# A decoder layer on one core: two softmax copies moved to ScalarE, FFN weights loaded within the attention, last sums closed in PSUM

## The chip, the core and the metric

The kernel runs on one core of one Trainium2 chip. The metric is the device time of one execution in microseconds. The engines are TensorE (PE; its weight loads are PEld), VectorE (DVE), ScalarE (ACT), GpSimd (POOL) and SyncE (SP), which here issues nearly all DMAs. [...]

## The reference

Two batches of 512 tokens, D = 1024, all in float32. Three sublayers, each followed by a layer norm over the sum with its input:

```python
# 1. causal attention over a window of 128: 32 query heads, 8 kv heads, head size 128
s = einsum("bhgnd,bhmd->bhgnm", q, k) / sqrt(128)      # masked: j <= i and i - j < 128
o = softmax(s) @ v;  x = layernorm(x + o @ wo.T)
# 2. fake-quantised product with the context (8 bits, scale s, zero point z)
fq(x) = (clip(round(x / s + z), 0, 255) - z) * s
x = layernorm(x + fq(x) @ fq(ctx))
# 3. FFN with ternary weights, 2752 inner features
inter = silu(gate(x / 128)) * up(x / 128)
q = int8(trunc(clip(inter * 128, -128, 127)))
x = layernorm(x + int8(trunc(clip(down(q) * 128, -128, 127))))
```

## The kernel before

**Order.** The code is written as generators that are stepped from each other (`between` in `attention` and `feed_forward`, classes `Background` for work in the background); a framework then places every instruction in its engine's queue by expected readiness and adds the waits. Up to eight DMAs are in flight on SP, in eight lanes.

**Strassen.** Projections, output projection and gate/up products are done as seven products of half-size blocks. `strassen_left` (L87) makes sums of the weights (L93 to L96), `strassen_right` (L73) sums of the activations (L80 to L83); its third difference overwrites a quarter of its input. `strassen` (L100) runs products 1, 6, 2, 7, 5, 4, 3 of four matmuls each (L109); product 1 is copied by ACT (L115), product 2 as well (L121), the others are added by DVE (L118 to L134).

**Attention (L166), per batch and kv head group g, 16 groups.** While group m's four token tiles are worked, the projections of group m + 1 are stepped in between. A tile takes: scores of four heads (`scores`, L268) into PSUM tile `ps`, the 128 keys of the tile before and its own; DVE copies the earlier keys (L284) and copies its own under the mask (L285), takes the maximum (L289), ACT the exponent with its sum (L293), DVE scales (L299). `transpose_p` (L302): PE transposes the weights into PSUM tile `pt` (L305), DVE multiplies them by the mask keep_cur (L311, part of the own keys) and by keep_prev (L312, part of the earlier keys). `weigh` (L317): two matmuls into `o` (L319, L321), ACT copies to `oT` (L325). After four tiles `keep` (L327) makes Strassen sums `oS` on DVE (L333 to L336) and stores them with five DMAs in `kept` (L340).

**In the background of the attention.** The sums of the output weights (`sum_output_weights`, L801, 32 steps) and of the gate/up weights (`sum_weights`, L826, 42 steps): a step loads a tile (two buffers), makes four sums on DVE into a tile `s`, and stores that with one DMA to DRAM (L823, L853). In batch 1's attention the output projection of batch 0 (`project_out`, L365, matmuls `y` at L412) and the cross attention of batch 0 (`Cross`, L441, with `quantise`, L470) run too.

**FFN (L540).** 21 units of 128 inner features and a rest of 64, for each batch. A unit loads its weights (`load_factors`, L561: two DMAs of weights, one of sums) and its down weights (`load_down`, L582, split in `split`, L590, into hi and lo of type f32r), makes gate and up by Strassen, `activate` (L598), and every second unit adds its down products (L656) to `acc` in SBUF on DVE (L662). Output and cross attention of batch 1 run in the background of batch 0's FFN. After the rest unit (`rest_unit`, L627) `finish` (L666) does each of four tiles: x is loaded back from DRAM (L671, one buffer fin_x) for batch 0, then ACT Abs and Sign (L676, L677), DVE (L679 to L684), ACT Square (L687), the root (L48), ACT scale (L693), output DMA (L694). The last two units (21st and rest) of batch 1 run in two halves of 256 tokens (L723 to L738).

Of the kernel before, what the change touches and what calls it, by code (L numbers as in the profile page):

```python
# [18 lines left out]
P = 128  # L19
# [3 lines left out]
D = 1024  # L23
# [49 lines left out]
def strassen_right(nc, pool, x, name):  # L73

    b11, b12, b21, b22 = (x[:, ts(k, KH), ts(n, NH)] for k in range(2) for n in range(2))
    t = pool.tile([P, 3, KH, NH], F32, tag="t", name=name)
    t1, t2, t4 = (t[:, k] for k in range(3))
    nc.vector.tensor_tensor(t1, b12, b11, ALU.subtract)  # L80
    nc.vector.tensor_tensor(t2, b22, t1, ALU.subtract)
    nc.vector.tensor_tensor(b12, b22, b12, ALU.subtract)
    nc.vector.tensor_tensor(t4, b21, t2, ALU.subtract)  # L83
    return b11, b21, b22, t4, t1, t2, b12
# [81 lines left out]
def attention(nc, tc, consts, xbuf, tpool, ps_p, dram, kept, complete, between):  # L166
# [3 lines left out]
    ident, mask_i, keep_cur, keep_prev = consts  # L170
    xT_d, wq_d, wk_d, wv_d = dram
    with ExitStack() as ctx:
# [44 lines left out]
        qT, kT, vT, v = {}, {}, {}, {}  # L217
# [34 lines left out]
        def transpose_v(b, g):  # L252
            ps = ps_t.tile([P, TPB, P], F32, tag="t", name=f"vtr_{b}_{g}")
            for i in range(TPB):
                nc.tensor.transpose(ps[:, i, :], vT[b, g][:, ts(i, P)], ident)
            v[b, g] = kvpool.tile([P, TPB, P], F32, tag="v", name=f"v_{b}_{g}")
            nc.scalar.copy(v[b, g], ps)

# [9 lines left out]
        def scores(b, g, i):  # L268
# [12 lines left out]
            if i == 0:  # L281
                nc.gpsimd.memset(s, MASKED)
            else:
                nc.vector.tensor_copy(s, ps[:, :, 0:P])  # L284
# [17 lines left out]
        def transpose_p(b, g, i, s):  # L302
            ps = ps_t.tile([P, G, P], F32, tag="t", name=f"pt_{b}_{g}_{i}")
            for h in range(G):
                nc.tensor.transpose(ps[:, h, :], s[:, h, :], ident)  # L305
            cur = work.tile([P, G, P], F32, tag="cur", name=f"cur_{b}_{g}_{i}", bufs=1)
            if i == 0:
                nc.vector.tensor_copy(cur, ps)
                return cur, None
            prev = work.tile([P, G, P], F32, tag="prev", name=f"prev_{b}_{g}_{i}", bufs=1)  # L310
            nc.vector.tensor_tensor(cur, ps, keep_cur.unsqueeze(1).to_broadcast([P, G, P]), ALU.mult)  # L311
            nc.vector.tensor_tensor(prev, ps, keep_prev.unsqueeze(1).to_broadcast([P, G, P]), ALU.mult)  # L312
            return cur, prev
# [3 lines left out]
        def weigh(b, g, i, cur, prev):  # L317
            ps = ps_o.tile([P, G, P], F32, tag="o", name=f"o_{b}_{g}_{i}")
            nc.tensor.matmul(ps, v[b, g][:, i, :], cur, start=True, stop=prev is None)  # L319
            if prev is not None:  # L320
                nc.tensor.matmul(ps, v[b, g][:, i - 1, :], prev, start=False, stop=True)  # L321
            if i == 0:
                outputs[b, g] = work.tile([P, 4, 2, NH], F32, tag="oT", name=f"oT_{b}_{g}")
            half, place = divmod(i, 2)
            nc.scalar.copy(outputs[b, g][:, ts(half, 2), :, ts(place, P)], ps.rearrange("p (k j) t -> p k j t", k=2))  # L325

        def keep(b, g):  # L327

            o = outputs[b, g]
            a11, a12, a21, a22 = (o[:, k] for k in range(4))  # L330
            t = work.tile([P, 3, 2, NH], F32, tag="oS", name=f"oS_{b}_{g}", bufs=1)
            s4, s1, s2 = (t[:, k] for k in range(3))
            nc.vector.tensor_tensor(s1, a21, a22, ALU.add)  # L333
            nc.vector.tensor_tensor(s2, s1, a11, ALU.subtract)
            nc.vector.tensor_tensor(a21, a11, a21, ALU.subtract)
            nc.vector.tensor_tensor(s4, a12, s2, ALU.subtract)  # L336
            to = kept[b]
            for k, src in ((slice(0, 2), o[:, 0:2]), (slice(3, 4), o[:, 3:4]), (slice(4, 6), t[:, 1:3]),
                           (slice(6, 7), o[:, 2:3]), (slice(2, 3), t[:, 0:1])):
                nc.sync.dma_start(out=to[:, k, g], in_=src)  # L340
# [3 lines left out]
        for m, (b, g) in enumerate(groups):  # L344
# [4 lines left out]
            for i in range(TPB):  # L349
# [4 lines left out]
                cur, prev = transpose_p(b, g, i, s)  # L354
# [3 lines left out]
                weigh(b, g, i, cur, prev)  # L358
# [181 lines left out]
def feed_forward(nc, tc, xres, spill, x2T, tpool, gate_up, wd_d, pools, out, between):  # L540

    wgu_d, rest_d, sums = gate_up
    raw_pool = pools[1]
    with ExitStack() as ctx:
# [16 lines left out]
        def load_factors(u):  # L561

            m = units[u][1]
            w = wbig.tile([P, 7, KH, P], F32, tag="wbig", name=f"wgu_{u}")
            if m == NCHUNK:
                rest = w.rearrange("p a c i -> p (a c) i")[:, :KC]
                nc.sync.dma_start(out=rest, in_=rest_d)
                return rest
            nc.sync.dma_start(out=w[:, 0:2], in_=wgu_d[m, :, 0].rearrange("p (j c) i -> p j c i", j=2))
            nc.sync.dma_start(out=w[:, 2], in_=wgu_d[m, :, 1, KH:])  # L570
            nc.sync.dma_start(out=w[:, 3:7], in_=sums[m])
            return [w[:, k] for k in (0, 1, 6, 2, 3, 4, 5)]

        def load_tail():
# [5 lines left out]
            left[u + 1] = load_factors(u + 1)  # L580
# [67 lines left out]

        def down(us, i, e):
# [4 lines left out]
            parts = [(acts[v], half) for v in us for half in halves[v]]  # L654
            for k, (act, half) in enumerate(parts):
                nc.tensor.matmul(ps, act[:, ts(i, P)], half[:, ts(e, HALF)], start=k == 0, stop=k == len(parts) - 1)  # L656
# [6 lines left out]
            if us[-1] % PER == NCHUNK and e == 1:  # L663
                finish(t)

        def finish(t):  # L666

            y = acc[t]
            if t in spill:
                x = work.tile([P, D], F32, tag="fin_x", name=f"fin_x_{t}", bufs=1)  # L670
                nc.sync.dma_start(out=x, in_=spill[t])  # L671
            else:
                x = xres[t]
            a = wdp.tile([P, D], F32, tag="wd", name=f"fin_{t}", bufs=1)
            r = raw_pool.tile([P, D], F32, tag="raw", name=f"fin_r_{t}")
            nc.scalar.activation(a, y, AF.Abs, scale=128.0)  # L676
            nc.scalar.activation(y, y, AF.Sign)  # L677

            nc.vector.tensor_scalar(r, a, 128.0, RND, ALU.min, ALU.add)  # L679
            nc.vector.scalar_tensor_tensor(a, r, RND, a, ALU.subtract, ALU.is_gt)  # L680
            nc.vector.scalar_tensor_tensor(r, r, RND, a, ALU.subtract, ALU.subtract)
            nc.vector.tensor_tensor(r, r, y, ALU.mult)
# [4 lines left out]
            nc.scalar.activation(y, x, AF.Square, bias=mean, accum_out=total)  # L687
# [8 lines left out]
        left[0] = load_factors(0)  # L696
        right, todo = {}, []
        for u, (b, m) in enumerate(units[:split_at]):
            load_down(u)
            if u + 1 < split_at:  # L700
                left[u + 1] = load_factors(u + 1)
            else:
                load_tail()
            if m == 0:
                right[b] = strassen_right(nc, tpool, x2T[b], f"t2_{b}")
            if m == NCHUNK:
                rest_unit(u, b)
# [15 lines left out]
        for h in range(2):  # L723
            where = [(i, e) for i in range(h * TPB // 2, (h + 1) * TPB // 2) for e in range(2)]
            for u in range(split_at, len(units)):
                if h == 0:
                    load_down(u)
                if u == len(units) - 1:
                    rest_unit(u, 1, h)
                else:  # L730
# [3 lines left out]
                    todo = []  # L734
                if h == 0:
                    split(u)
            for i, e in where:
                down((split_at, split_at + 1), i, e)  # L738
# [3 lines left out]
def decoder_layer(ctx, tc, x, xT, ctx_kv, wq, wk, wv, wo, s1, z1, s2, z2, wgu, wgu_rest, wd, out):  # L742
# [25 lines left out]
    keep_prev = const.tile([P, P], F32, tag="keep_prev", name="keep_prev")  # L768
    nc.gpsimd.affine_select(
        out=keep_prev, in_=ones, compare_op=ALU.is_gt, fill=0.0, base=0, pattern=[[-1, P]], channel_multiplier=1  # L770
    )
# [18 lines left out]
    x2T, sums, complete = {}, [], set()  # L790
    wo_sums = scratch.tile([P, 4, NKV, 2, HALF], F32, tag="wo_sums", name="wo_sums")
# [9 lines left out]
    def sum_output_weights(pool):  # L801
# [10 lines left out]
        for n, (g, j, q) in enumerate(steps):  # L812
# [4 lines left out]
            t = pool.tile([P, 4, Q4], F32, tag="s", name=f"wo_sum_{g}_{j}_{q}")  # L817
            t4, t1, t2, t3 = (t[:, k] for k in range(4))
            nc.vector.tensor_tensor(t1, b12, b11, ALU.subtract)
            nc.vector.tensor_tensor(t2, b22, t1, ALU.subtract)  # L820
            nc.vector.tensor_tensor(t3, b22, b12, ALU.subtract)
            nc.vector.tensor_tensor(t4, b21, t2, ALU.subtract)
            nc.sync.dma_start(out=wo_sums[:, :, g, j, ts(q, Q4)], in_=t)  # L823
            yield

    def sum_weights(pool):  # L826
# [13 lines left out]
        for n, (m, k) in enumerate(steps):  # L840
# [6 lines left out]
            s = pool.tile([P, 4, 2, P], F32, tag="s", name=f"sum_{m}_{k}")  # L847
            s1_, s2_, s3_, s4_ = (s[:, q] for q in range(4))
            nc.vector.tensor_tensor(s1_, a21, a22, ALU.add)
            nc.vector.tensor_tensor(s2_, s1_, a11, ALU.subtract)  # L850
            nc.vector.tensor_tensor(s3_, a11, a21, ALU.subtract)
            nc.vector.tensor_tensor(s4_, a12, s2_, ALU.subtract)
            nc.sync.dma_start(out=sums[m][:, :, k : k + 2], in_=s)  # L853
            yield

    def in_attention(b, g, i):
# [8 lines left out]
        if calls[0] % 3 == 0:  # L865
            aside.step()
        if calls[0] % 3 == 0 and (b or g or i):
# [3 lines left out]

    calls = [0]
    with tc.tile_pool(name="s_prep", bufs=2) as prep, tc.tile_pool(name="ps_y", bufs=2, space=PSUM) as ps_y:
        ahead.add(sum_output_weights(prep))
        ahead.add(sum_weights(prep))
        attention(nc, tc, (ident, mask_i, keep_cur, keep_prev), xbuf, tpool, pools[3],
                  (xT, wq, wk, wv), kept, complete, in_attention)
        aside.drain()
        ahead.drain()

# [5 lines left out]

    aside.add(cross.context(1))
    aside.add(cross_tokens(1))
    feed_forward(nc, tc, xres, spill, x2T, tpool, (wgu, wgu_rest, sums), wd, pools, out, in_feed_forward)
# [50 lines left out]
```

## Time and profile before

| | us |
|---|---|
| median of 3 runs | 2054.29 (2053.85 to 2056.23) |
| profiled execution | 2049.04 |
| its span | 2047.2 |
| PE busy in the span | 1963.9 |
| DVE busy | 1238.8 |
| ACT busy | 479.8 |
| mean DMA rate | 210 GB/s |

Stages in the trace: attention of batch 0 to about 500 us, of batch 1 to 1102, FFN of batch 0 to about 1660, its four finishes to 1735 beside the FFN of batch 1, which goes to 1999, then the tail. The profile is of one execution; times are from the start of its span. A group of instructions is one line and operation: busy time, mean duration in ns, then the idle time of its engine just before it and what ended that. A matmul of float32 is two passes on PE, so two records; 512 columns take 0.43 us a pass.

### The profile page before, as it was taken

The numbers are of one execution on the slowest core, as the hardware profiler recorded it, in microseconds if no ns is written. First come the engines' busy times: TensorE is split into PE (matmuls) and PEld (weight loads), VectorE is DVE, ScalarE is ACT, GpSimd is POOL, SyncE is SP. The second block draws the span as 40 slices with busy tenths as digits, with TensorE's granted clock in tenths as the row PEclk, the third lists the DMA queues.
The fourth block names the chain that finished last, engine by engine and source line by source line (L and its number), as shares of the span: only waits on it lengthen the run. The fifth ranks groups of instructions, "written<-read, shape, count | busy, mean of one in ns | idle before, by whom it ended". The sixth has DMA issues, their size and how long they took to land.

```text
span 2047.2 us, 21954 instructions
## 1 busy us (share of the span) xinstructions
PE 1963.9 (96%) x8016; PEld 1441.6 (70%) x8016; DVE 1238.8 (61%) x2435; ACT 479.8 (23%) x1121; POOL 14.4 (1%) x35
## 2 busy tenths in 40 slices
PE   8999999999999999999997999999999999999993
PEld 5877777778666666667774666666678877888882
DVE  5888787787334345345774443633467687666667
ACT  1222212222111122112332211211123245221224
POOL 0000000000000000000000000000000000000000
PEclk9999999999999999999998999999999999999997
DMA  8998887875466655655249865667733345534421
GB/s 286 323 321 286 258 264 242 279 239 183 180 251 227 223 213 216 235 213 188 108 152 323 307 248 213 245 223 261 257 113 122 126 147 193 192 132 149 149 83 41
DMA packets 218826, 430.57 MB, mean 210 GB/s; under 512 B 15072, under 2 KB 149216, under 8 KB 199008
## 3 DMA queue, kind: packets, MB, share of 16 engines
q1 hardware_dynamic: 217568, 427.09, 59.8%
q10 hardware_dynamic: 1152, 2.10, 0.3%
q8 instruction: 63, 1.03, 0.2%
q14 instruction: 43, 0.35, 0.0%
HBM read 354.68 MB, written 74.45 MB: 210 GB/s over the span
## 4 chain that ended last, share of the span: by engine, by line
PE 75%; DMA 12%; DVE 9%; SPq 2%; issue 1%; ACT 1%; DVEq 0%; ACTq 0%
PE prod L109 39%; PE y L412 17%; PE d L656 8%; PE ps L277 3%; DMA w<-in_wq_dram 3%; DMA or<-wo_sums 2%; PE o L319 2%; DMA raw<-in_wgu_dram 2%; PE o L321 1%; PE m L525 1%; DMA w<-in_wv_dram 1%; PE pt L305 1%; DMA or<-in_wo_dram 1%; SPq L836 1%; DMA wgu<-sums 1%
## 5 line engine op out<-in xcount | busy, mean ns | idle before, releaser
L412 PE MATMUL y<-or,ol 128*128 128x512 f32 x896 | 406.9, 595 | 16.9 <-DMA wgu<-in_wgu_dram 10.8
L109 PE MATMUL prod<-x2T,wgu 128*128 128x256 f32 x1312 | 304.6, 380 | 0.1
L412 PEld LDWEIGHTS y<-or,ol 128*128 128x128 f32 x896 | 167.4, 190 | 189.9 <-issue 173.8
L109 PEld LDWEIGHTS prod<-x2T,wgu 128*128 128x128 f32 x1312 | 249.3, 191 | 47.3 <-issue 13.1
L109 PE MATMUL prod<-xT,w 128*128 128x256 f32 x1128 | 268.9, 382 | 7.1 <-ACT st L115 6.5
L109 PEld LDWEIGHTS prod<-xT,w 128*128 128x128 f32 x1128 | 211.0, 191 | 46.1 <-ACT st L115 10.6
L109 PE MATMUL prod<-t,wgu 128*128 128x256 f32 x984 | 231.2, 379 | 3.4 <-DMA wgu<-sums 2.8
L109 PEld LDWEIGHTS prod<-t,wgu 128*128 128x128 f32 x984 | 186.3, 190 | 41.4 <-issue 15.3
L109 PE MATMUL prod<-t,s 128*128 128x256 f32 x752 | 180.2, 380 | 1.3 <-DVE kT L134 1.2
L656 PE MATMUL d<-hi,act 128*128 128x512 f32 x352 | 153.5, 436 | 10.8 <-DVE act L621 10.7
L109 PEld LDWEIGHTS prod<-t,s 128*128 128x128 f32 x752 | 141.1, 190 | 27.0 <-issue 5.2
L656 PE MATMUL d<-lo,act 128*128 128x512 f32 x352 | 140.3, 399 | 0.0
L293 ACT ACTIVATE s<-s,top 128x128 f32<-128x128 f32 x256 | 99.6, 390 | 173.2 <-DVE top L290 173.0
L662 DVE TENSOR_TENSOR acc<-d,acc 128x512 f32<-128x512 f32 x160 | 110.1, 690 | 49.2 <-PE d L656 48.9
L124 DVE TENSOR_TENSOR st<-prod,st 128x256 f32<-128x256 f32 x88 | 37.0, 420 | 126.9 <-PE prod L109 126.5
L277 PE MATMUL ps<-kT,qT 128*128 128x256 f32 (+1 forms) x512 | 111.6, 354 | 0.0
L277 PEld LDWEIGHTS ps<-kT,qT 128*128 128x128 f32 x512 | 88.5, 190 | 28.9 <-issue 17.5
L594 ACT CAST hi<-wd 128x1024 fp32r<-128x1024 f32 x44 | 46.0, 1047 | 266.9 <-PE d L656 167.6
L325 ACT COPY oT<-o 128x512 f32<-128x512 f32 x64 | 37.4, 584 | 277.7 <-PE o L321 163.9
L656 PEld LDWEIGHTS d<-hi,act 128*128 128x128 f32 x352 | 66.8, 190 | 48.9 <-DVE acc L662 21.3
L284 DVE COPY s<-ps 128x512 f32<-128x512 f32 x48 | 33.0, 687 | 99.4 <-PE ps L277 99.3
L109 PE MATMUL prod<-t,w 128*128 128x256 f32 x376 | 89.8, 381 | 2.8 <-DVE st L124 2.8
(184 smaller groups left out, 2223.2 us busy)
## 6 DMA issues: line engine op xcount, KB each, us to landing
or<-wo_sums SPq DMA_DIRECT2D x64, 1024.0 KB, 5.2
or<-in_wo_dram SPq DMA_DIRECT2D x48, 1024.0 KB, 5.5
wgu<-sums SPq DMA_DIRECT2D x41, 1024.0 KB, 7.4
w<-in_wq_dram SPq DMA_DIRECT2D x64, 512.0 KB, 4.7
ol<-kept SPq DMA_DIRECT2D x112, 256.0 KB, 2.9
raw<-in_wgu_dram SPq DMA_DIRECT2D x168, 128.0 KB, 3.8
sums<-sum SPq DMA_DIRECT2D x42, 512.0 KB, 4.1
wd<-in_wd_dram SPq DMA_DIRECT2D x42, 512.0 KB, 3.7
```

The source lines that it names most:

```text
L109: nc.tensor.matmul(ps, left[k - 1][:, c, :], right[k - 1][:, c, :], start=start and c == 0, stop=c == KH - 1, skip_group_check=True)
L124: nc.vector.tensor_tensor(u3, two, p1, ALU.add)
L277: nc.tensor.matmul(ps[:, h, :width], qT[b, g, h][:, ts(i, P)], kT[b, g][:, lo : lo + width], start=True, stop=True,)
L284: nc.vector.tensor_copy(s, ps[:, :, 0:P])
L293: nc.scalar.activation(s[:, h, :], s[:, h, :], AF.Exp, bias=top[:, h : h + 1], scale=QSCALE, accum_out=total[:, h : h + 1],)
L305: nc.tensor.transpose(ps[:, h, :], s[:, h, :], ident)
L319: nc.tensor.matmul(ps, v[b, g][:, i, :], cur, start=True, stop=prev is None)
L325: nc.scalar.copy(outputs[b, g][:, ts(half, 2), :, ts(place, P)], ps.rearrange("p (k j) t -> p k j t", k=2))
L412: nc.tensor.matmul(ps, left[:, c // 2, c % 2], right[:, c // 2, c % 2], start=k in (1, 6, 5) and s == 0 and c == 0, stop=s == LAST and c == 3,
L594: nc.scalar.copy(hi, raw[u])
L656: nc.tensor.matmul(ps, act[:, ts(i, P)], half[:, ts(e, HALF)], start=k == 0, stop=k == len(parts) - 1)
L662: nc.vector.tensor_tensor(acc[t][:, ts(e, HALF)], ps, acc[t][:, ts(e, HALF)], ALU.add)
```

## The change

- `scores`: the copy of the earlier keys goes to ACT. `transpose_p`: instead of the product with keep_prev, ACT copies the whole of `pt` to `both`; `weigh` takes v of the tile before times `both` plus (v of this tile less v of the tile before, `vd`) times `cur`. The mask keep_prev is gone; `vd` is made once a group on DVE.
- `strassen_right` writes its third difference in a tile of its own; the input stays whole.
- The sums of the weights: one of the four is written over the loaded tile, and each store is split into two DMAs.
- The attention output of a group is two tiles, one for each half of the tokens.
- The weights of the FFN's first unit are loaded within the attention of batch 1, into the buffer of xT, and strassen_right of batch 0's FFN input is called there too. Before the first units of batch 1 the background queues are drained and batch 1's sums are made ahead of the rest unit.
- `finish` gets x and its sums handed in, x comes into the two buffers `right`, and Sign, rounding and comparison are in BF16 tiles.
- In the two last halves the sum is closed in PSUM: an identity matmul brings `acc` in, the 21st unit's down products are added ahead, the rest unit's come last, and `finish` reads PSUM.

```diff
 def strassen_right(nc, pool, x, name):
-    t = pool.tile([P, 3, KH, NH], F32, tag="t", name=name)
+    t = pool.tile([P, 4, KH, NH], F32, tag="t", name=name)
...
-    nc.vector.tensor_tensor(b12, b22, b12, ALU.subtract)
+    nc.vector.tensor_tensor(t3, b22, b12, ALU.subtract)
...
             v[b, g] = kvpool.tile([P, TPB, P], F32, tag="v", name=f"v_{b}_{g}")
             nc.scalar.copy(v[b, g], ps)
+            vd[b, g] = kvpool.tile([P, TPB - 1, P], F32, tag="vd", name=f"vd_{b}_{g}")
+            nc.vector.tensor_tensor(vd[b, g], v[b, g][:, 1:], v[b, g][:, : TPB - 1], ALU.subtract)
...
-                nc.vector.tensor_copy(s, ps[:, :, 0:P])
+                nc.scalar.copy(s, ps[:, :, 0:P])
...
-            prev = work.tile([P, G, P], F32, tag="prev", name=f"prev_{b}_{g}_{i}", bufs=1)
+            both = work.tile([P, G, P], F32, tag="both", name=f"both_{b}_{g}_{i}", bufs=1)
             nc.vector.tensor_tensor(cur, ps, keep_cur.unsqueeze(1).to_broadcast([P, G, P]), ALU.mult)
-            nc.vector.tensor_tensor(prev, ps, keep_prev.unsqueeze(1).to_broadcast([P, G, P]), ALU.mult)
+            nc.scalar.copy(both, ps)
...
+                nc.tensor.matmul(ps, v[b, g][:, i - 1, :], both, start=True, stop=False)
+                nc.tensor.matmul(ps, vd[b, g][:, i - 1, :], cur, start=False, stop=True)
...
+            if place == 0:
+                outputs[b, g, half] = work.tile([P, 2, 2, NH], F32, tag=f"oT{half}", name=f"oT_{b}_{g}_{half}", bufs=2 - half)
...
+def load_factors(nc, w, gate_up, m):
...
+    nc.sync.dma_start(out=w[:, 0:2], in_=wgu_d[m, :, 0].rearrange("p (j c) i -> p j c i", j=2))
+    nc.sync.dma_start(out=w[:, 2], in_=wgu_d[m, :, 1, KH:])
+    nc.sync.dma_start(out=w[:, 3:7], in_=sums[m])
+    return [w[:, k] for k in (0, 1, 5, 2, 3, 4, 6)]
...
             if us[-1] % PER == NCHUNK and e == 1:
-                finish(t)
+                x = stream.tile([P, 2, 2, HALF], F32, tag="right", name=f"fin_x_{t}").rearrange("p a b c -> p (a b c)")[:, :D]
                 nc.sync.dma_start(out=x, in_=spill[t])
+                finish(t, x, [acc[t]])
+
+        def finish(t, x, sums):
             a = wdp.tile([P, D], F32, tag="wd", name=f"fin_{t}", bufs=1)
-            r = raw_pool.tile([P, D], F32, tag="raw", name=f"fin_r_{t}")
-            nc.scalar.activation(a, y, AF.Abs, scale=128.0)
-            nc.scalar.activation(y, y, AF.Sign)
-            nc.vector.tensor_scalar(r, a, 128.0, RND, ALU.min, ALU.add)
-            nc.vector.scalar_tensor_tensor(a, r, RND, a, ALU.subtract, ALU.is_gt)
-            nc.vector.scalar_tensor_tensor(r, r, RND, a, ALU.subtract, ALU.subtract)
-            nc.vector.tensor_tensor(r, r, y, ALU.mult)
+            rm = raw_pool.tile([P, 2, D], BF16, tag="raw", name=f"fin_r_{t}")
+            r, m = rm[:, 0], rm[:, 1]
+            sign = b_work.tile([P, D], BF16, tag="a1", name=f"fin_s_{t}", bufs=1)
+            for k, y in enumerate(sums):
+                part = ts(k, D // len(sums))
+                nc.scalar.activation(a[:, part], y, AF.Abs, scale=128.0)
+                nc.scalar.activation(sign[:, part], y, AF.Sign)
+            nc.vector.tensor_scalar(r, a, RND, RND, ALU.add, ALU.subtract)
+            nc.vector.tensor_tensor(m, r, a, ALU.is_gt)
+            nc.vector.tensor_tensor(r, r, m, ALU.subtract)
+            nc.vector.scalar_tensor_tensor(r, r, 128.0, sign, ALU.min, ALU.mult)
...
             if m == NCHUNK:
+                finish_between()
+                right[b + 1] = strassen_right(nc, tpool, x2T[b + 1], f"t2_{b + 1}")
                 rest_unit(u, b)
...
+                    rest_unit(u, 1, h)
+                    for k, (i, e) in enumerate(where):
+                        pool, tag = (ps_d, "d") if k < 2 else (ps_p, "p")
+                        ps[i, e] = pool.tile([P, HALF], F32, tag=tag, name=f"d_{h}_{k}")
+                        nc.tensor.matmul(ps[i, e], ident, acc[TPB + i][:, ts(e, HALF)], start=True, stop=False)
+                        down_parts(ps[i, e], [split_at], i, e, False, False)
...
             for i, e in where:
-                down((split_at, split_at + 1), i, e)
+                down_parts(ps[i, e], [split_at + 1], i, e, False, True)
+                if e == 1:
+                    finish(TPB + i, xres[TPB + i], [ps[i, 0], ps[i, 1]])
...
-            nc.vector.tensor_tensor(t3, b22, b12, ALU.subtract)
+            nc.vector.tensor_tensor(b12, b22, b12, ALU.subtract)
             nc.vector.tensor_tensor(t4, b21, t2, ALU.subtract)
-            nc.sync.dma_start(out=wo_sums[:, :, g, j, ts(q, Q4)], in_=t)
+            nc.sync.dma_start(out=wo_sums[:, 0:3, g, j, ts(q, Q4)], in_=t)
+            nc.sync.dma_start(out=wo_sums[:, 3, g, j, ts(q, Q4)], in_=b12)
...
-            nc.vector.tensor_tensor(s3_, a11, a21, ALU.subtract)
+            nc.vector.tensor_tensor(a21, a11, a21, ALU.subtract)
             nc.vector.tensor_tensor(s4_, a12, s2_, ALU.subtract)
-            nc.sync.dma_start(out=sums[m][:, :, k : k + 2], in_=s)
+            nc.sync.dma_start(out=sums[m][:, 0:3, k : k + 2], in_=s)
+            nc.sync.dma_start(out=sums[m][:, 3, k : k + 2], in_=a21)
...
             aside.step()
+            if b and g == NKV - 1 and (0, "tokens") in complete and not early:
+                prepare_feed_forward()
...
+    def prepare_feed_forward():
+        w = xbuf.tile([P, 7, KH, P], F32, tag="x1", name="wgu_0")
+        early.append(load_factors(nc, w, gate_up, 0))
+        early.append(strassen_right(nc, tpool, x2T[0], "t2_0"))
...
+    def finish_between():
+        behind.drain()
+        aside.drain()
```

In the changed kernel the copy for `scores` is L285, the scaling L300, `both` L313, Abs and Sign of `finish` L691 and L692, its DVE steps L694 to L699, Square L702, its last ACT step L708, the adds to `acc` L676, and the copy of product 1 L114.

## The prediction

> **What bounds the kernel now.** I read the page first: its span, its busy times and its slices.
>
> ```profile
> span 2047.2 us, 21954 instructions
> PE 1963.9 (96%) x8016; PEld 1441.6 (70%) x8016; DVE 1238.8 (61%) x2435; ACT 479.8 (23%) x1121; POOL 14.4 (1%) x35
> ...
> PEclk9999999999999999999998999999999999999997
> ```
>
> TensorE sets the time: it idles only 83 of 2047 us. None of the edits takes matmul work away (the tail adds some), so only those holes can give anything. Adding up the idle stretches in the trace gives 5.5 us at the start, 63.0 in gaps and 20.2 after the last matmul, out and end included. Where they lie, from the windows view (span, then busy PE, PEld, DVE, ACT, POOL with counts, PEclk, DMA share, GB/s):
>
> ```profile
> 100.00:200.00 100.00, 96.64 (x442) 78.26 (x441) 82.89 (x187) 25.23 (x87) 1.05 (x2) 1.00 0.92 304
> 200.00:300.00 100.00, 93.08 (x424) 73.50 (x423) 80.52 (x181) 20.22 (x76) 0.52 (x1) 1.00 0.82 260
> 500.00:700.00 200.00, 200.00 (x731) 133.12 (x730) 77.35 (x147) 26.60 (x98) 1.05 (x2) 1.00 0.58 211
> 1100.00:1200.00 100.00, 88.24 (x304) 57.73 (x303) 42.65 (x68) 20.24 (x28) 0.00 (x0) 0.95 0.80 288
> 2000.00:2047.00 47.00, 16.64 (x58) 12.06 (x56) 33.69 (x73) 22.32 (x32) 0.00 (x0) 0.69 0.11 45
> ```
>
> In the first attention (to 500 us) PE misses 3 to 7 us per 100 while DVE is about 80% busy and the DMA engines 70 to 92%; in the second (500 to 1100) almost nothing is missing. Then come one hole at 1102 and the tail. The chain of waits across 1102 (start, us, what):
>
> ```profile
> 1102.02 0.59 ACT oT L325
> ...
> 1105.29 3.53 DMA kept<-oS
> 1108.82 0.02 issue
> 1108.84 0.03 SPq L569
> 1108.86 0.03 issue
> 1108.89 3.78 DMA wgu<-in_wgu_dram
> 1112.67 0.10 issue
> 1112.77 2.04 PE y L412 x2
> ```
>
> The last head's output is stored, and only behind that store does SP issue the first FFN weights: PE stands 10.79 us.
>
> **Early FFN weights (and boundary order): about -10.** Trace first: after the gap, one y matmul (two passes, 0.86 us elsewhere) and one product (1.73) take from 1112.77 to 1117.18, 4.41 instead of 2.59: 1.8 lost. So this place costs 12.6. The Trainium skill, "TensorE: Matmul & The Clock Gate" (Part 1), says that an idle window of some 3.4 us halves the clock until about as long has been worked. By it a rest below 3.4 us is free of that charge. The row agrees: after a 2.12 us gap at 1709.9, 14 matmuls took 3.26 us (14 x 0.216 is 3.02).
> In the changed order unit 0's weights are issued on SP within the last group, and its first products are mixed with the last tiles. After the last o matmul PE has ready: a product (1.73), a y step (3.43), four products (6.9): 12.1 us. Unit 1's weights still queue on SP behind the last stores. DVE has two quantise steps of raw_5 (0.81, 0.69) ahead of or among the oS sums, so the last store goes at about 5.9 instead of 3.3, lands 3.5 later, then wd and wgu: 9.5, plus 3.8 to 4.5 of landing, 13.3 to 14.1. Rest 1.2 to 2.0, with hand-overs 2 to 2.7 and no clock loss. Gain 12.6 - 2.5 = 10 (8 to 12; by the rule 1.8 less if the rest passes 3.4). The three loads moved early stand on SP some 16 places ahead of that group's first stores; their buffer (x1) held batch 1's xT, last read at 1059, so they wait for nothing then. Batch 0's strassen_right (four of 1.22 on DVE) stood at 1058 to 1066 before too: nothing.
>
> **Tail: about -3.** The act of the last half is ready at 2021.1. Before, eight more passes, the adds and Abs follow, and DVE's L679 starts at 2025.89. After, four f32r matmuls (0.43 each at the low clock) close tile 6 at 2022.9, half-width Abs/Sign (0.63 each) feed L694 at about 2024, and one add (0.69) no longer stands in the DVE chain: 1.9 + 0.6 = 2.5. Added: 8 identity matmuls x 0.86 = 6.9 us of PE; they lie in the gaps of 4.43 and 5.88 before 2013.55 and 2021.16, where PE waits for DVE's act. Uncovered they would cost 3.4 per half. BF16 in finish: the nearest rows (1.21 to 1.22 for L680 to L684) give nothing. The skill's "VectorE: DVE Perf Modes" (the perf-mode tier table) lets a tensor_tensor with all operands of 16 bits run twice as fast, which fits only L696: 0.5 per tile, up to 2.1 over four tiles. No run here shows it; I take a quarter, as other steps of the chain are on ACT. Sum 3 (0 to 5).
>
> **Finish of tiles 0 to 3, after unit 21: about +7.** Before, each tile waits for the one fin_x buffer, whose reload waits for the output's landing; that spreads the four tiles over 1662 to 1735 and costs PE 5 to 7 us there. With two reload buffers the tiles pack together. In ACT's changed order, between unit 22's g copy and the copy of product 1 of unit 23 (which PE's next accumulation needs) stand four Abs and four Sign (8 x 1.06), two Square (2 x 1.34), three table loads (3 x 1.28), two L708 (2 x 1.24), sigmoid, Abs and Sign of unit 22 (1.9): 19.8 us against 7.1 before. DVE has the matching chain. PE's work from the rest unit's start to where it needs that copy: 6.9 + 12.1 + 7.4 + 5.2 + 1.7 = 33.3 us; the finish chain begins when the first sums close and reaches the copy at about 42. Stall 8 to 9.4, plus some 2 of low clock and 1 to 2 of small waits, less the 5 to 7 saved: loss 7. Bounds: a gain of 3 if the chain keeps up, a loss of 10.
>
> **Softmax on ScalarE: about -8.** From the groups by form (busy, mean ns; idle before, releaser):
>
> ```profile
> L284 DVE COPY s<-ps 128x512 f32<-128x512 f32 x48 | 33.0, 687 | 99.4 <-PE ps L277 99.3
> L312 DVE TENSOR_TENSOR prev<-pt,keep_prev 128x512 f32<-128x512 f32 x48 | 32.6, 680 | 0.0
> L93 DVE TENSOR_TENSOR s<-w 128x512 f32<-128x512 f32 x47 | 32.4, 690 | 54.2 <-DMA w<-in_wv_dram 27.7 <-DMA w<-in_wq_dram 26.4
> ```
>
> DVE loses 48 x 0.687 (L284) and 48 x 0.680 (L312), 65.6 us; it gains 16 vd subtractions of 384 columns (between 0.42 and 0.69, say 0.55), 9. Net 57, half of it in the first attention: from 78 to 72% busy. ACT gains 96 x 0.584, 56 us, at 20% busy. `both` waits for DVE's cur on the same PSUM tile, so o starts 0.8 later than with prev; behind it on ACT stand oT and the next exp. PE has at least 1.7 us of other work between pt and o in nearly every tile: nothing, but up to 5 if a few lack it. Gaps named after softmax (`pt` behind L299) sum to 11; of the 20 us of gaps in 100 to 500 I take 8 (2 to 14).
>
> **Sums in place: about +8.** The fourth difference overwrites the loaded tile, so each of 74 steps issues a second store, and the buffer's next load waits for its landing. In SP's changed order about 50 such loads stand three DMAs or fewer behind their store (none before): SP stands still, and w, wo and raw loads queue behind it. DVE then waits at L93 or at the sums, with softmax behind it; it already waits 54 us for w (last row above). Replaying one stretch by hand (store 4.1, load 4.8, three sums 1.3, issue 0.4) gives 22 us for four steps, 5.5 each, if DVE takes each at once; queued on DVE about 6.5. Before, the 74 steps ran from 22 to 482 us, 6.2 each; the changed order ends them near 507, 6.55 each. So it is on the edge: 8, between 0 and 26.
>
> **x2T kept whole:** the same four DVE operations into one tile more; batch 1's four (4.9 us) now stand ahead of the rest unit, where PE has its 6.9: nothing.
>
> **Sum:** -10 - 3 + 7 - 8 + 8 = -6. The profiled execution took 2049.04 (span 2047.2), so 2043; the median of the runs lies 5.25 above it, so 2048.
>
> **Rivals.** *A, everything shows:* DVE relief 14, sums free, finish even, boundary 11, tail 4: 29, so 2025. For it: PE's holes lie exactly where DVE is full. Against it: the SP queue and ACT's 19.8 us. *C, the finish eats the boundary:* the rest at the boundary is 4 to 5 with its clock loss, so 6 gained there, 3 in the tail, and the pile-up costs 10: about 2055, no change. *B, slower:* the two-buffer turn of the weight sums becomes the pace of the first attention. Place: 22 to 520 us, SP. Each step at 6.8 instead of 6.55 stretches it by 74 x 0.25 = 18; DVE's relief of 8 then repays nothing: 2054.3 - 13 + 7 + 18 = 2066. It decides from about 6.63 per step (74 x 0.08 eats the 6 gained). For it: DMA share 0.92 and landings of 4 to 6 us already. Against it: 5.5 if nothing queues. *That ACT only takes over what PE waits for* is in the low end of the 8.
>
> **Numbers.** Forecast (2039 to 2050) 0.35; A 0.16; C 0.17; B 0.32. A measurement tells about 0.2%, 4 us, from no change: faster 0.51, same 0.17, slower 0.32. The range 2026 to 2068 reaches into A and B, and leaves out half of A's lower part and B's tail, about 2 in 10.
>
> **What would show it.** Boundary: the 10.8 us wait before y at 1102 gone, a wait of 2 to 3 for wgu of unit 1. Finish: one PE wait of 8 or more behind ACT st in unit 23. Tail: no adds at the end, about 3 us shorter after the last rest unit. Attention: DVE near 72% to 500 us, fewer gaps behind L300; if B, long DVE waits for wo, raw and w, and the last sum well past 507. I am wrong if ACT's added copies make pt or o late, or if the sums set the pace.

## The result and the profile after

| | before | after |
|---|---|---|
| median, us | 2054.48 (2047.81 to 2060.79, 12 runs) | 2054.68 (2045.03 to 2059.53, 12 runs) |
| profiled execution | 2049.04 | 2045.03 |
| its span | 2047.2 | 2043.0 |

The ratio is 0.9995 with an interval of 0.9978 to 1.0012: -1 us, give or take 3.5. A second measurement (run c1 below) gave 1.0000 (0.9989 to 1.0010). So the change made no difference that can be measured. The profiled execution of after is its fastest of twelve; its 4 us less are not the verdict, but its stages can be compared.

The page of after, same rows as shown of before:

```profile
span 2043.0 us, 22124 instructions
PE 1968.4 (96%) x8022; PEld 1444.1 (71%) x8032; DVE 1183.1 (58%) x2347; ACT 531.5 (26%) x1223; POOL 14.2 (1%) x34
...
PEclk9999999999999999999999999999999999999998
```

DVE has 56 us less work and ACT 52 more, as the diff says, and TensorE's busy time is up by 4.5. The dip of the clock at the boundary (the 8 in the middle of before's row) is gone. The windows of after (span, busy PE, PEld, DVE, ACT, POOL with counts, PEclk, DMA share, GB/s), with 1600 to 1700 added; the last line is 1600 to 1700 of before:

```profile
100.00:200.00 100.00, 95.07 (x433) 75.89 (x432) 77.36 (x176) 30.97 (x97) 0.53 (x1) 1.00 0.89 290
200.00:300.00 100.00, 94.35 (x433) 75.36 (x433) 72.91 (x164) 26.81 (x88) 1.05 (x2) 1.00 0.78 251
1100.00:1200.00 100.00, 97.43 (x338) 62.58 (x337) 45.16 (x73) 23.36 (x39) 0.00 (x0) 1.00 0.80 299
1600.00:1700.00 100.00, 91.33 (x386) 72.83 (x386) 77.49 (x144) 44.20 (x64) 1.94 (x3) 0.97 0.41 141
2000.00:2043.00 43.00, 20.80 (x84) 15.25 (x82) 27.96 (x67) 25.63 (x43) 0.31 (x1) 0.80 0.12 50
...
1600.00:1700.00 100.00, 98.60 (x426) 78.98 (x425) 76.12 (x131) 37.03 (x53) 1.93 (x3) 1.00 0.37 127
```

Read the first two rows against before: DVE fell from 82.89 and 80.52 to 77.36 and 72.91, and PE's two rows together stayed as they were (96.64 and 93.08 before, 95.07 and 94.35 now). At 1100 PE gained 9 us. At 1600 it lost 7 (98.60 before), and its clock fell from 1.00 to 0.97.

By stage, from marks that both programs have (first attention: to the last `o` of batch 0; then to the last `o` of batch 1; to the rest unit of FFN batch 0; to the 21st unit of batch 1; to the end):

| us | before | after | difference |
|---|---|---|---|
| first attention | 493.1 | 495.2 | +2.1 |
| second attention | 608.9 | 612.7 | +3.8 (3.5 are products of unit 0, moved in) |
| boundary and FFN of batch 0 | 542.9 | 531.3 | -11.6 |
| its finish, FFN of batch 1 | 331.5 | 338.4 | +6.9 |
| 21st unit and tail | 70.8 | 65.5 | -5.3 |
| sum (of the unrounded stages) | 2047.2 | 2043.0 | -4.2 |

These are single executions, but the profiles of the runs below agree on most stages: the finish took 337.0 to 338.4 us in all eight with two x buffers and 330.3 to 331.6 in the four with one, the end 65.5 to 66.3 wherever it has the changed form. The first attention does not repeat so well: in six executions with the changed kernel's code in that stretch it ended at 495.2 (after), 497.3, 498.6, 500.5 (c1), 503.1 and 506.0. So its +2.1 says nothing.

The boundary in the timeline of after (start, us, instruction, idle time before it and what ended that), TensorE only:

```profile
1106.80 1.02 PE L326 MATMUL o<-cur,vd 128*128 128x512 f32 x2
1107.66 1.89 PE L108 MATMUL prod<-x2T,wgu 128*128 128x256 f32 x8
1109.39 3.60 PE L418 MATMUL y<-or,ol 128*128 128x512 f32 x8
1112.82 5.34 PE L108 MATMUL prod<-t,wgu 128*128 128x256 f32 x24
1118.00 1.89 PE L108 MATMUL prod<-x2T,wgu 128*128 128x256 f32 x8
1121.83 1.53 PE L108 MATMUL prod<-x2T,wgu 128*128 128x256 f32 x6 [1.94 <-DMA wgu<-in_wgu_dram]
```

Products of unit 0 fill the place where PE stood 10.79 us, and 1.94 us remain, for unit 1's weights. Later, in the finish:

```profile
1669.67 2.75 PE L108 MATMUL prod<-t,wgu 128*128 128x256 f32 x12
1673.50 1.97 PE L108 MATMUL prod<-x2T,wgu 128*128 128x256 f32 x8 [1.08 <-DMA wgu<-in_wgu_dram]
1681.48 3.43 PE L108 MATMUL prod<-x2T,wgu 128*128 128x256 f32 x8 [6.01 <-ACT st L114]
```

The 6.01 us wait for ACT's copy `st`, and the eight matmuls behind it take 3.43 instead of 1.89. ACT at that time, without a pause:

```profile
1674.36 1.04 ACT L691 ACTIVATE fin<-acc 128x1024 f32<-128x1024 f32 x1
1675.31 1.23 ACT L708 ACTIVATE fin_x<-fin_x,shift,ln_r 128x1024 f32<-128x1024 f32 x1
1676.55 1.28 ACT L48 ACT_TABLE_LOAD   x1
...
1679.42 1.23 ACT L708 ACTIVATE fin_x<-fin_x,shift,ln_r 128x1024 f32<-128x1024 f32 x1
1680.56 0.62 ACT L627 ACTIVATE g_None<-g_None 128x512 f32<-128x512 f32 x1
1681.08 0.35 ACT L114 COPY st<-prod 128x256 f32<-128x256 f32 x1
```

The copy of 0.35 us stands behind two tiles' finish. What SP's queue waited for in the first 500 us of after (`SPq`, line of the DMA that waited, what it waited for: total, times, longest):

```profile
SPq L858 <- DMA sums<-raw: 67.8, 27, 6.2
SPq L829 <- DMA wo_sums<-wo: 36.7, 21, 4.9
```

A load of `raw` or `wo` waits until the store out of the same buffer has landed. These two are 104.5 us; all of SP's waits for a DMA come to 127.4 us in this stretch, to 20.9 in before. The last weight sum ends at 518.3 instead of 483.3. And DVE's longest waits there that are not for a transfer's data, with the row of before for the same place:

```profile
DVE s L286 <- ACT s L285: 19.1, 15, 3.0
...
DVE s L284 <- PE ps L277: 11.4, 7, 3.0
```

In before the copy stood on DVE itself, and DVE waited there for PE's scores. Now it waits for ACT's copy of them.

### The profile page after: what moved, and what is told of

Its sections match the earlier page's. It is cut to its first block, busy times and chain, and to the rows that moved or that the text cites. A ratio compares the mean times of both kernels' runs of the same rounds, so it can differ in the third digit from the quotient of the medians.

```text
span 2043.0 us, 22124 instructions
## 1 busy us (share of the span) xinstructions
PE 1968.4 (96%) x8022; PEld 1444.1 (71%) x8032; DVE 1183.1 (58%) x2347; ACT 531.5 (26%) x1223; POOL 14.2 (1%) x34
## 3 DMA queue, kind: packets, MB, share of 16 engines
q8 instruction: 64, 1.05, 0.2%
## 5 line engine op out<-in xcount | busy, mean ns | idle before, releaser
L108 PE MATMUL prod<-t,wgu 128*128 128x256 f32 x1312 | 304.0, 379 | 0.3 <-DVE st L123 0.3
L108 PEld LDWEIGHTS prod<-t,wgu 128*128 128x128 f32 x1312 | 248.7, 190 | 51.2 <-issue 17.2
L108 PE MATMUL prod<-x2T,wgu 128*128 128x256 f32 x984 | 232.0, 382 | 10.0 <-ACT st L114 7.0
L108 PEld LDWEIGHTS prod<-x2T,wgu 128*128 128x128 f32 x984 | 186.9, 191 | 44.4 <-issue 8.8
L108 PE MATMUL prod<-xT,w 128*128 128x256 f32 x752 | 183.2, 383 | 8.4 <-ACT st L114 6.3
L108 PE MATMUL prod<-t,w 128*128 128x256 f32 x752 | 182.2, 385 | 9.4 <-DVE st L123 6.2
L108 PEld LDWEIGHTS prod<-t,w 128*128 128x128 f32 x752 | 142.8, 192 | 34.2 <-DVE st L123 8.9
L108 PEld LDWEIGHTS prod<-xT,w 128*128 128x128 f32 x752 | 139.8, 192 | 36.6 <-ACT st L114 9.5
L676 DVE TENSOR_TENSOR acc<-d,acc 128x512 f32<-128x512 f32 x152 | 105.0, 692 | 45.0 <-PE d L662 44.8
L286 DVE COPY_PREDICATED s<-mask_i,ps 128x512 f32<-128x512 int32 x64 | 46.7, 729 | 123.4 <-ACT s L285 120.2
L123 DVE TENSOR_TENSOR st<-prod,st 128x256 f32<-128x256 f32 x88 | 37.1, 421 | 125.9 <-PE prod L108 125.5
```

Of the source, the lines that this page charges most:

```text
L108: nc.tensor.matmul(ps, left[k - 1][:, c, :], right[k - 1][:, c, :], start=start and c == 0, stop=c == KH - 1, skip_group_check=True)
L123: nc.vector.tensor_tensor(u3, two, p1, ALU.add)
L286: nc.vector.copy_predicated(s, mask_i.unsqueeze(1).to_broadcast([P, G, P]), ps[:, :, width - P : width])
L676: nc.vector.tensor_tensor(acc[t][:, ts(e, HALF)], ps, acc[t][:, ts(e, HALF)], ALU.add)
```

## The experiments

Runs with the same value of before in the table were measured on the same chip; across chips the ratios are compared. The theory was that the changed kernel loses by the sums written in place (S) and by packing the finishes together (P) what it gains at the boundary and in the tail. The rival was the softmax split. Measured, in microseconds:

| run | what | median | before | ratio, interval |
|---|---|---|---|---|
| e1 | sums in a tile of their own | 2042.04 | 2052.07 | 0.9948 (0.9927 to 0.9968) |
| e2 | both copies on DVE | 2045.91 | 2052.07 | 0.9968 (0.9951 to 0.9985) |
| e3 | one x buffer in finish | 2045.06 | 2052.07 | 0.9959 (0.9944 to 0.9975) |
| e4 | early load, call moved | 2050.74 | 2052.07 | 1.0002 (0.9983 to 1.0021) |
| c1 | changed kernel again | 2053.63 | 2053.60 | 1.0000 (0.9989 to 1.0010) |
| e5 | first weights in the FFN's pool | 2066.43 | 2053.60 | 1.0060 (1.0039 to 1.0080) |
| e6 | e1 and e3 | 2036.09 | 2053.60 | 0.9914 (0.9893 to 0.9935) |
| e7 | e6 and e2 | 2031.72 | 2053.60 | 0.9891 (0.9871 to 0.9912) |
| e8 | three tiles only | 2059.81 | 2052.46 | 1.0022 (1.0008 to 1.0036) |
| e9 | adds back in the tail | 2056.02 | 2052.46 | 1.0012 (1.0001 to 1.0024) |
| e11 | old softmax, e1, e3 | 2041.98 | 2052.46 | 0.9937 (0.9914 to 0.9961) |

**e1, the sums apart.** As before, one store; to have room, the third difference of `strassen_right` overwrites its input again. In that form, which e1, e6, e7 and e8 share with the kernel before, the rest units and the 21st unit of the tail read this difference where a quarter of their input (half the features, half the tokens) should stand, so what they compute there is not the reference's. The changed kernel, and e11, leave the input whole.

```diff
-            t = pool.tile([P, 3, Q4], F32, tag="s", ...)
+            t = pool.tile([P, 4, Q4], F32, tag="s", ...)
-            nc.vector.tensor_tensor(b12, b22, b12, ALU.subtract)
+            nc.vector.tensor_tensor(t3, b22, b12, ALU.subtract)
```

> The changed kernel with the weight sums as before: all four in a tile of their own, one store a step. To make room strassen_right keeps three tiles and its third difference overwrites a quarter of its input again, so the rest units and the 21st unit of the tail read that quarter replaced, as in the kernel before. Theory S (the waits of SP for the stores of the in-place sums ate what DVE's relief gave in the first attention): the first attention, which ended at 495.2 us in the changed kernel and 493.1 before, ends at 485 to 489, and the time falls by 6 to 10 us. Theory R (PE's small holes there follow neither DVE's load nor SP's waits for the stores): it ends at 493 to 497, the time stays within 3 us of the changed kernel's; SP's waits for stores (104 us) vanish and nothing else does.

It is 9 to 10 us faster than the changed kernel (8.7 below e4 on the same chip, 0.47% by the ratios). SP's waits for a DMA fell from 127.4 to 21.4 us; the longest waits of its queue are again for the engines that read or write the tiles:

```profile
SPq L195 <- PE prod L109: 42.9, 18, 15.1
SPq L344 <- ACT oT L331: 25.8, 8, 5.7
SPq L845 <- DVE wo_sum L842: 18.2, 4, 6.6
```

The last sum ends at 464, the first attention at 492.4 (497.3, 499.0 and 503.1 in e4, e2 and e3). By the time S holds. The end of the first attention did not come down to the 485 to 489 expected of S, though it lies below all six of the changed kernel's code. And e1 also changes `strassen_right`.

**e8, three tiles.** Only that part of e1.

> The changed kernel with three tiles in strassen_right alone (the third difference overwrites a quarter of its input, so the rest units and the 21st unit of the tail read that quarter replaced, as in the kernel before). The kernel with the sums apart had this too. Theory (it moves nothing, the sums alone gave that kernel's 10 us): within 3 us of the changed kernel's 2054, first attention ending at 495 to 503. Rival (the space or the order it frees gave part of it): 5 to 10 us faster.

No gain: it is even 0.2% above before, slower than was expected, with the first attention at 504.6. So e1's gain belongs to the sums.

**e2, both copies on DVE.**

```diff
-                nc.scalar.copy(s, ps[:, :, 0:P])
+                nc.vector.tensor_copy(s, ps[:, :, 0:P])
-            nc.scalar.copy(both, ps)
+            nc.vector.tensor_copy(both, ps)
```

> The changed kernel with its two copies (of the scores' earlier keys and of the transposed weights) on DVE again, the rest as it is. Theory S (DVE's load counts in the first attention, the relief was only eaten elsewhere): DVE goes from 74 to about 81% busy in the first 500 us, its end moves from 495 to 501 to 504, the time grows by 6 to 10 us. Theory R: DVE gets as busy, but the end stays at 493 to 498 and the time within 3 us.

Not slower: 4.8 below e4, with intervals that touch. DVE is back at 78% from 100 to 500 us (73% in after), and nothing is lost. So the part of the theory by which DVE's relief is worth time fell.

**e3, one x buffer.** x of the finishes goes through a single buffer instead of two.

```diff
-                    x = stream.tile([P, 2, 2, HALF], F32, tag="right", ...)
+                    x = stream.tile([P, KC, N], F32, tag="x0", ...)
```

> The changed kernel with one buffer for the x that finish loads back (a dead tile of the first batch's input) in place of two. Theory P (the two buffers let four finishes pack together ahead of the copy of product 1 on ACT): the PE gap of 6.0 us behind that copy falls below 3, from the first rest product to the 21st unit of the tail it takes 331 to 334 us (338.4 in the changed kernel, 331.5 before), the time falls by 4 to 7. Rival: the pile-up comes from draining the background and making batch 1's sums ahead of the rest unit, so the stretch stays at 337 to 339 and the time within 2 us.

The 6.0 us wait is gone, the stage of the finish takes 330.8 (338.4 in after), and the whole 7 us less (0.36% by the ratios). The window of e3:

```profile
1600.00:1700.00 100.00, 98.16 (x425) 78.86 (x424) 74.83 (x126) 35.58 (x54) 1.94 (x3) 1.00 0.40 137
```

PE has 98.16 instead of 91.33, at a clock of 1.00. In the first 60 us from the rest unit's start, which e3 reaches 12 us later, ACT is busy 30.8 us instead of 35.1. With one buffer each tile waits for the store of the one before (the second tile's x is issued at 1690.55, when the first tile's output landed), and that wait keeps ACT's queue open for the FFN.

**e4 and e5, where the early load counts.** e4 takes out the call that prepares the FFN within the last group; e5 loads unit 0's weights into the FFN's own pool.

```diff
-        w = xbuf.tile([P, 7, KH, P], F32, tag="x1", name="wgu_0")
-        early.append(load_factors(nc, w, gate_up, 0))
...
+        load_unit(0)
```

> The changed kernel without the load of the first FFN unit's weights and without strassen_right within the attention: both come after it. Theory (the early weights are what fills PE behind the last o): a gap of 9 to 12 us behind the last o matmul is back, with a low clock after it, and the time grows by 8 to 11 us. Rival (the gain at that place came from other moves, such as the halves of oT): the gap stays below 5 us and the time within 3.

> The changed kernel with the first FFN unit's weights in the FFN's own pool, whose space is the attention's until it ends; strassen_right stays in the attention. Theory B (what fills PE behind the last o is the place of the weights: a buffer outside the attention's pools, wherever the load is called): the load goes back behind the last stores, the gap behind the last o is 9 to 13 us again with a low clock after it, the time 8 to 12 us above the changed kernel's. Rival (the changed oT tiles and the order of the stores made the gap short): gap below 5 us, time within 3.

e4 missed: the load is still issued at 1067.65, when its buffer is free, so the place of the call does not decide it. In e5 the wait is back, for the attention's output `ol`, which is stored and loaded back; unit 0's weights are issued behind the last stores, at 1123.51:

```profile
1111.76 1.02 PE L418 MATMUL y<-or,ol 128*128 128x512 f32 x2
1125.46 2.07 PE L418 MATMUL y<-or,ol 128*128 128x512 f32 x2 [12.68 <-DMA ol<-kept]
```

12.8 us above c1. What makes the load early is a buffer that does not belong to the pools which open when the attention's close.

**e6 and e7, the gains together.** e6 joins e1 and e3; e7 also has e2's copies.

> The weight sums apart (and three tiles in strassen_right, so that the rest units and the 21st unit of the tail read a quarter replaced, as in the kernel before) together with the one x buffer in finish. If the two losses are separate, their gains add up: first attention to 489 to 494 us, PE gap behind the copy in unit 23 below 1.5 us, 15 to 18 us below the changed kernel, 2033 to 2037 us. If one merely moved the other's, no more than 11.

> As the kernel with sums apart and one x, with the two softmax copies on DVE again (a quarter replaced as there). Theory L (DVE's load counts once the sums no longer hold SP up): 5 to 8 us slower than that kernel, and the first attention ends 4 to 8 us later. Theory R (it counts nowhere): within 3 us of it.

e6 is 17.5 below c1, e7 21.9 below c1 and 1.1% (0.9 to 1.3) below before: it beats both kernels, with DVE as full as in before:

```profile
PE 1967.8 (97%) x8022; PEld 1443.2 (71%) x8032; DVE 1237.0 (61%) x2443; ACT 481.8 (24%) x1131; POOL 14.2 (1%) x34
```

e7 is 4.4 below e6, again with touching intervals; neither theory had it faster. With the changed kernel's form of the softmax, the copies are worth nothing or a little less than nothing on ACT.

**e9, the tail.** The last two units' down products are added to `acc` by DVE again, the rest of the tail as changed.

```diff
-                        nc.tensor.matmul(ps[i, e], ident, acc[TPB + i][:, ts(e, HALF)], start=True, stop=False)
...
+                down((split_at, split_at + 1), i, e)
```

> The changed kernel with the end as before: the down products of the last two units are summed in PSUM only over those two, DVE adds them to acc, finish reads acc; BF16 in finish stays. Theory (closing the sums in PSUM gave the tail's gain, BF16 little): from the start of the 21st unit of the tail to the end it takes 69 to 71 us (65.5 in the changed kernel, 70.8 before), the time grows by 4 to 5. Rival (BF16 gave it): it takes 65 to 67, the time within 2.

From the 21st unit to the end 68.0 us: 70.8 before, 65.5 after. Its gaps behind `act` on PE are 4.68 and 4.33 where after has 0.20 and 1.71. So closing in PSUM is worth 2.5, the rest of the tail's edits 2.8. That is between what was expected of the theory (69 to 71) and of the rival. The whole time says little here: the changed kernel was not measured on this chip, and e8 beside it is slower still.

**e11, before's softmax with the good parts.** The masks as in before, the sums apart, one x, the FFN input whole.

> The changed kernel with the softmax of the kernel before (both steps on DVE, prev and keep_prev, no vd), the weight sums apart and one x in finish; strassen_right keeps its input whole. Nothing is left out or replaced. If neither the copies' engine nor the whole input counts, it takes 2030 to 2036, as the kernel with its copies on DVE (2031.7) and the one with them on ACT (2036.1) do. If the copies on ACT do help once the sums are apart, it takes 2038 or more.

Faster than both kernels by 0.6%, but in the range (2038 or more) that was set down for the case that the copies on ACT do help. Against e6 (0.9937 and 0.9914, intervals that overlap) the changed softmax would gain 5 us. But e7, which has both copies on DVE as e11 has, is the fastest (0.9891), so the engine of the copies is not what holds e11 back. What is left between e11 and e7 is the form of the softmax (two mask products, or one product, a copy and `vd`), the input kept whole, and the chip. Of the 9.6 us between their profiles, 4.2 lie in the FFN of batch 0, where no softmax runs. Why stays open. Of the kernels here that leave the input whole, e11 is the fastest by the ratios.

## Why the prediction was right or wrong

The time lies within the range, but at -1 instead of -6 the likeliest sign did not come. One sum at the start is off: the 63.0 us of gaps already hold the 5.5 at the start (83.2 = 63.0 + 20.2). No term rests on it.

- **Boundary, -10: right.** 1.94 us remain, in the 1.2 to 2.0 foreseen, for the transfer foreseen; PEclk is 1.00 there. From the trace 12.6 - 2.4 = 10.2 (the rest and a later wait of 0.46); e5 puts the whole at 12.8. Two errors offset each other in the rest: unit 1's weights were issued 7.8 us behind the last `o`, not 9.5, and took 5.8 to land, not 3.8 to 4.5. And the chain shown of before names the wrong transfer. The `y` matmul that ended the 10.79 us reads `ol`, issued at 1107.39 and landed 5.2 us later, 0.1 before it; the weights, issued at 1108.89, landed 5.2 later too, after it had begun. PE needed both, and the early weights give it work that waits for neither. The rule of the Trainium skill weighed there ("TensorE: Matmul & The Clock Gate", Part 1) fits: no charge behind 1.94, but 8 matmuls in 3.43 behind the 6.01 at 1681.
- **Finish, +7: right in mechanism, the size with luck.** +6.9 by stage, and e3 gives it back (330.8, before 331.5). The stall was 6.01 plus 1.08 where 8 to 9.4 was worked out, and before lost 3.6 us to waits in the 95 us from the rest unit on, where 5 to 7 was taken. (The terms listed for ACT's 19.8 add up to 19.4.)
- **Sums in place, +8: right in mechanism and size.** e1: 9 to 10. SP's waits for its own stores of the sums are 104.5 of the 127 us. What they did on DVE is seen in one place:

```profile
321.93 0.43 DVE L871 TENSOR_TENSOR sum<-raw 128x256 f32<-128x256 f32 x1 [3.26 <-issue]
...
324.94 0.42 DVE L123 TENSOR_TENSOR st<-prod,st 128x256 f32<-128x256 f32 x1
...
325.40 1.61 PE L108 MATMUL prod<-t,w 128*128 128x256 f32 x4 [2.17 <-DVE st L123]
```

  The load of `raw` was issued at 317.07, when the store out of its buffer had landed. The sum at L871 stood 3.26 us until `raw` was there, the product add of L123 is queued behind it, and PE has a gap of 2.17 until that is done. PE's gaps behind such adds go with the sums, as the last column of the table below shows. The pace came to 6.7 a step (22.8 to 518.3, 74 steps), above the 6.63 from which the slower rival was to decide. The price set on that pace was wrong: the last sums slid past the end of the first attention (495), and PE was not stretched to their pace.
- **Tail, -3: mis-sized.** -5.3. The PSUM part was 2.5 as worked out. The term that failed is the rest, "I take a quarter" of BF16's 2.1, 0.5 against 2.8 for all that e9 leaves. L696 did become fast, the mixed and scalar forms did not:

```profile
L695 DVE TENSOR_TENSOR fin_r<-fin_r,fin 128x1024 bf16<-128x1024 bf16 x8 | 9.8, 1224 | 0.2
L697 DVE SCALAR_TENSOR_TENSOR fin_r<-fin_r,fin_s 128x1024 bf16<-128x1024 bf16 x8 | 9.8, 1223 | 0.2
...
L696 DVE TENSOR_TENSOR fin_r<-fin_r 128x1024 bf16<-128x1024 bf16 x8 | 5.5, 688 | 0.1
```

  (L695 reads `fin`, which is float32.) The tier table of the Trainium skill ("VectorE: DVE Perf Modes") holds for L696: all its operands are of 16 bits, and it takes 688 ns against 1214 before. In the last half two such steps stand one after the other on DVE (2025.89 and 2031.26 in after), which makes about 1.05 us there, an estimate. e9 does not part BF16 from the other edits.
- **Softmax on ACT, -8: failed.** e2 and e7 put the move of the copies between nothing and 5 us of loss. The step that failed is "of the 20 us of gaps in 100 to 500 I take 8": DVE's share fell from 78 to 72% of the first 500 us as foreseen, but PE's gaps do not follow DVE's load. Without the start they are 25.9 us in the first 505 in before and 27.0 in after. By what ended them:

| us | copies | sums | behind the scaled softmax (`pt`) | behind product adds (`st`) |
|---|---|---|---|---|
| before | DVE | apart | 11.0 | 3.2 |
| after | ACT | in place | 7.8 | 8.3 |
| c1 | ACT | in place | 9.2 | 10.8 |
| e2 | DVE | in place | 10.8 | 6.0 |
| e1 | ACT | apart | 12.0 | 3.1 |
| e6 | ACT | apart | 12.3 | 2.0 |
| e7 | DVE | apart | 9.8 | 3.3 |
| e11 | DVE | apart | 12.0 | 4.3 |

  The column that the relief should have lowered follows neither: 7.8 to 12.3 with the copies on ACT, 9.8 to 12.0 on DVE. The trace offers a reason, in the means of the 24 tiles of batch 0 that have a tile before them. From the last score to the scaled weights it takes 6.42 us where before took 6.89, since DVE now waits for ACT's copy `s`. And `both`, which waits for `cur` on the same PSUM tile, starts `o` 2.88 behind the end of `pt` instead of 2.44. Together 9.30 against 9.33: the tile takes as long as it did. In e6 and e7, which differ in the copies alone, it is 9.33 and 9.37. That such chains, and not DVE's load, set PE's gaps is argued from these means; no run shortened one.

Added up: boundary -10 to -13, tail -5, finish +7, sums +9 to +10, copies 0 to +5, so between -2 and +7, against -1 (3.5 either way). The form of the softmax is not in this sum; by e11 it could be a gain of some us. That the time stayed in the range is in part luck: the softmax missed by 8 or more, and the tail's and the boundary's larger gains made up for part of it.

The rival of no change gave the right sum, but not for its reason: the finish took 7, and the sums in place took as much again.

## What to carry to other kernels

Do not read an engine's busy share as what it costs: moving 56 us from the fullest helper engine bought nothing that could be measured, and a tile's way through softmax and transposition to its product stayed as long (9.30 us, 9.33 before). When a store leaves the very buffer that the next load needs, every transfer behind that load on SP's queue waits for the landing too; a tile for the result removed it here (127 to 21 us). And a wait that spreads work can be worth keeping: here one buffer more let two finishes fill ACT's queue ahead of a copy of 0.35 us that TensorE needed.

## What the runs showed of the hardware

ACT copies 128x512 of float32 out of PSUM in 587 ns (L285 and L313, 48 times each), DVE did it in 687 (L284 of before). A `scalar_tensor_tensor` of 128x1024 gained nothing from BF16 operands (1223 ns at L697, 1218 at L681 of before). A store out of a buffer and the next load into it cost SP up to 6.2 us of standing still at a time. And TensorE's clock fell behind a stand of 6.0 us (PEclk 0.97 in 1600 to 1700, 1.00 in e3 without that stand), not behind one of 1.9 (1.00 in 1100 to 1200).
